# Layer 1's softmax divided by query, bfloat16 transposes by DMA, and expert biases carried in the weights

## The chip, the cores and the metric

The kernel runs as one program on one core of one Trainium2 chip. The metric is the device time of one execution in microseconds; three plain runs before the change took 1664.41, 1665.76 and 1665.9 us (median 1665.76). One more execution was recorded by the hardware profiler; all durations below are from it.

A core has five engines with a queue each, which run in the order of their queues and wait for one another through semaphores: PE (TensorE: matrix products and transposes, results in PSUM), DVE (VectorE), ACT (ScalarE), POOL (GpSimd) and SP (which here only issues DMAs).

## What is computed

Two layers on x of 2 x 2048 x 512, each a cross-attention to a context of 128 tokens and a feed-forward part, with a layer norm ahead of each and a residual. Cut to what the change touches:

```python
def _L0_ffn_ref(x, clip_x, clip_down, w_gate, w_up, w_down):
    # weights and activations are rounded to 255 steps: exact in bfloat16
    ...
def _L1_xattn_ref(q, k, v, mask, Wq, bq, Wk, bk, Wv, bv, Wo, bo):
    scores = jnp.einsum('bhqd,bhkd->bhqk', Q, K) / math.sqrt(DV)      # 16 heads of 32
    scores = jnp.where(mask, jnp.asarray(1e-09, scores.dtype), scores)
    attn = jax.nn.softmax(scores, axis=-1)
    ctx = jnp.einsum('bhqk,bhkd->bhqd', attn, V)
    return ctx.transpose(0, 2, 1, 3).reshape(b, -1, H * DV) @ Wo.T + bo
def _L1_ffn_ref(x, Wg, bg, We, be):
    probs = jax.nn.softmax(x @ Wg + bg, axis=-1)
    idx = jnp.argmax(probs, axis=-1)                                  # the expert: idx % 8
    p = jnp.take_along_axis(probs, idx[..., None], axis=-1)[..., 0]
    h = jax.nn.relu(jnp.einsum('bsd,edf->besf', x, We) + be[None, :, None, :])
    ...                                                               # the chosen expert's h times p
x = x + _L0_xattn_ref(_layernorm(x), ctx_1024, ctx_1024, ...)
x = x + _L0_ffn_ref(_layernorm(x), ...)
x = x + _L1_xattn_ref(_layernorm(x), ctx_1024, ctx_1024, ...)
x = x + _L1_ffn_ref(_layernorm(x), ...)
```

## The kernel before

The 4096 rows of x lie in SBUF as 32 tiles of 128 rows (`xs[n]`, with four more columns in `xw[n]`). The work runs in stages, one behind the other, with some overlap.

**Layer 0's attention (30 to 700 us)** is a loop over 64 units, a unit being 256 rows and 4 of 16 heads; its order on PE, DVE and ACT is that of the code (`manual_schedule`). Beside it the feed-forward weights are loaded by SP, rounded on DVE (`quantised`, L263 to L269), and one unit later transposed ("turns"): `gate_up` (22 tiles of 128 x 512) and `down` (4 of 128 x 1408) transpose in blocks of 128 x 128 on PE (L284, L302) and copy from PSUM on ACT (L285, L303).

**The feed-forward part, first half (711 to 870 us)**: 8 blocks of 512 rows, in each 11 steps of eight bfloat16 matmuls of 512 columns (L711), a Silu on ACT, a product and a maximum on DVE (L719, L721), and a store of h to DRAM by SP (L722). Between the steps DVE rounds the next block's rows (`quantised_x`, L95 and L666), PE transposes them (`turned_x`, L674), and ACT copies them to `xqT` (L675). Only PE's order is written out by hand here; a planner orders the other engines. Ahead of the blocks the gate's and the experts' biases are split into three bfloat16 parts each (`beparts`), with a table `sel` that selects an expert's rows.

**The second half** loads h back by SP, rounds it and multiplies by `wdT` (L777). It ends inside the first tile of layer 1. From here on PE, DVE, ACT and POOL all follow the order of the code.

**Layer 1's tiles (958 to 1488 us)**: for each of 32 tiles n the loop calls, with layer 1's feed-forward gate some tiles behind:
- `weighed(n-1)`: DVE multiplies tile n-1's mixed values by the reciprocal sums, L897
- `scores(n)`: PE, 16 products of 32 rows (L833); DVE masks (L841) and takes maxima (L846), 8 heads ("a half") at a time
- `queries`: PE (L813) and a copy on ACT (L816), for a later block; half of it here and half below
- `exponentials(n)`: ACT, one instruction per head (L855); those of the first half also sum, by accumulator
- `projected(n-1)`: POOL adds the output bias (L902), PE projects (L905), DVE adds to x (L906)
- `normed2(n-1)`, `kept_keys(n+1)`, `normed` of a later tile: statistics on DVE (L83, L85), a power on POOL (L92), the centering on DVE (L95)
- `logits(n-2)`: PE adds the bias by one bfloat16 product (L927) and multiplies by `wgate` (L929); DVE takes the maximum (L931) and its index (L935)
- `summed(n)`: DVE sums the second half (L859) and takes reciprocals (L861), POOL spreads them to features (`rw`, L864)
- `gated(n-2)`: an exponential on ACT (L943), the choice of the expert on DVE (L947 to L951)
- `turned(n)`: PE transposes the exponentials in four groups (L107) to PSUM, ACT copies them (L874)
- `turned2(n-1)`: the same for the normed x (L922)
- `mixed(n)`: PE transposes `rw` (L883), multiplies the exponentials by the values (L887); ACT copies the transposed `rw` (L892)
- `turned1`, in every second tile: PE and ACT transpose the next block's two tiles

PSUM tiles of the tag "m" share four banks, so the transposed groups, the logits, the projections and the queries take turns there: an allocation waits for the fourth one before it. From tile 24 on, `routing` sorts the rows of the first 22 tiles by expert on DVE, in pieces between the tiles.

**The experts (1463 to 1655 us)**: 39 calls of `expert(j)` on 128 rows each: rows gathered by POOL (L1096), centered on DVE, transposed on PE and copied on ACT (L1110), the bias added by one bfloat16 product (L1120), four products by the expert's weights (L1122, each two passes), a Relu on ACT (L1125), an addition on DVE (L1126), a scatter by POOL (L1127). Two of the calls lie in the last two tiles.

Of the kernel before, what the change touches and what calls it, by code (L numbers as in the profile page):

```python
# [11 lines left out]
F32 = mybir.dt.float32  # L12
# [11 lines left out]
P = 128  # L24
# [11 lines left out]
NE = 8  # L36
# [6 lines left out]
NJA = NTA - (NE - 1)  # L43
NJB = NT - NJA + NE - 1
NOWHERE = float(2**20)
QMAX = 127.0
# [12 lines left out]
def two_layers(ctx: ExitStack, tc: tile.TileContext, a, out):  # L59
# [14 lines left out]
    minus_half = const.tile([P, 1], F32, name="minus_half")  # L74
    nc.vector.memset(minus_half, -0.5)

    xw = [xres.tile([P, DX], F32, name=f"x{n}") for n in range(NT)]
# [64 lines left out]
    with ExitStack() as l0:  # L142
# [135 lines left out]
        def gate_up(w, dst, scales, i):  # L278
            wb = quantised(w, scales[:, i : i + 1])

            def turn():
                pt = psm.tile([P, ND, P], BF16, name="ptb", tag="m")
                for c in range(ND):
                    nc.tensor.transpose(pt[:, c, :], wb[:, c * P : (c + 1) * P], identb)  # L284
                nc.scalar.copy(dst[:, :, i * P : (i + 1) * P], pt)  # L285

            return turn
# [6 lines left out]
        def down(w, j):  # L294
            wb = quantised(w, sd[:, j : j + 1])

            def turn():
                for i in range(0, NI, 4):
                    n = min(4, NI - i)
                    pt = psm.tile([P, 4, P], BF16, name="ptb", tag="m")  # L300
                    for c in range(n):
                        nc.tensor.transpose(pt[:, c, :], wb[:, (i + c) * P : (i + c + 1) * P], identb)  # L302
                    nc.scalar.copy(wdT[:, i : i + n, j * P : (j + 1) * P], pt[:, :n, :])  # L303

            return turn
# [241 lines left out]
    wgate = wa.tile([P, ND, D], F32, name="wgate")  # L547
    beparts = w1.tile([P, D], BF16, name="beparts")
    sel = w1.tile([P, NE + 1, P], BF16, name="sel")
    bq = wa.tile([P, ND], F32, name="bq")  # L550
# [49 lines left out]
    with ExitStack() as up:  # L600
# [67 lines left out]
        def turned_x(n):  # L668
            blk, t = divmod(n, NBF)
            if t == 0:  # L670
                xqTs[blk] = work.tile([P, ND, BF], BF16, name="xqT", bufs=2)
            pt = psm.tile([P, ND, P], BF16, name="ptx", tag="m")
            for c in range(ND):
                nc.tensor.transpose(pt[:, c, :], xqs[n][:, c * P : (c + 1) * P], identb)  # L674
            nc.scalar.copy(xqTs[blk][:, :, t * P : (t + 1) * P], pt)  # L675
# [3 lines left out]
        for n in range(NBF):  # L679
            turned_x(n)  # L680

        nc.vector.memset(beparts, 0.0)
        nc.vector.memset(ones1, 1.0)
        nc.vector.tensor_scalar(bq, bq, 1.0 / math.sqrt(DH1), None, ALU.mult)
        bparts = kv.tile([NE + 1, 3, D], BF16, name="bparts")
        brest = kv.tile([NE + 1, D], F32, name="brest")
        load(brest[:NE, :], a["L1_ffn_be"])
        load(brest[NE:, :], a["L1_ffn_bg"].rearrange("(o d) -> o d", o=1))
        for k in range(3):
            nc.vector.tensor_copy(bparts[:, k, :], brest)  # L690
            nc.vector.tensor_tensor(brest, brest, bparts[:, k, :], ALU.subtract)
        be_dram = dram.tile([3, NE + 1, D], BF16, name="be_dram")
        nc.sync.dma_start(out=be_dram.rearrange("k e d -> e k d"), in_=bparts)
        for k in range(3):
            load(beparts[16 * k : 16 * k + NE + 1, :], be_dram[k])
        rowi = kv.tile([P, 1], I32, name="rowi")
        nc.gpsimd.iota(rowi, pattern=[[0, 1]], base=0, channel_multiplier=1)
        nc.vector.tensor_scalar(rowi, rowi, 15, None, ALU.bitwise_and)
        rowf = kv.tile([P, 1], F32, name="rowf")
        nc.vector.tensor_copy(rowf, rowi)  # L700
        ei_ = kv.tile([P, NE + 1], I32, name="ei_")
        nc.gpsimd.iota(ei_, pattern=[[1, NE + 1]], base=0, channel_multiplier=0)
        nc.vector.tensor_scalar(sel, ei_.unsqueeze(2).to_broadcast([P, NE + 1, P]), rowf, None, ALU.is_equal)

# [77 lines left out]

    scs, xTs, qTs, keeps, ss_, sums, rw_, pTs_, mix, os_ = {}, {}, {}, {}, {}, {}, {}, {}, {}, {}
    xn1s = {}
# [64 lines left out]
    def exponentials(n):  # L849

        sums[n] = small.tile([P, 16], F32, name="sums")
        for half, (s, mx) in enumerate(ss_[n]):
            for h in range(8):
                accum = {} if half else {"accum_out": sums[n][:, h : h + 1]}
                nc.scalar.activation(s[:, h, :], s[:, h, :], AF.Exp, bias=mx[:, h : h + 1], **accum)  # L855

    def summed(n):

        nc.vector.tensor_reduce(sums[n][:, 8:], ss_[n][1][0], AX.X, ALU.add)  # L859
        rs = small.tile([P, 4, 4], F32, name="rs")  # L860
        nc.vector.reciprocal(rs, sums[n].rearrange("p (r c) -> p c r", c=4))  # L861

        rw_[n] = mid.tile([P, 4, P], F32, name="rw", bufs=1)
        nc.gpsimd.tensor_copy(  # L864
            rw_[n].rearrange("p c (r f) -> p c r f", f=DH1), rs.unsqueeze(3).to_broadcast([P, 4, 4, DH1])
        )

# [9 lines left out]
    def mixed(n):  # L877

        b, pTs = n // TPB, pTs_[n]
        pr = psm.tile([P, 4, P], F32, name="pr1", tag="m")  # L880
        po = psm.tile([P, 4, P], F32, name="po1", tag="m")
        for c in range(4):
            nc.tensor.transpose(pr[:, c, :], rw_[n][:, c, :], ident)  # L883
        for c in range(4):
            for r in range(4):
                h = 4 * c + r
                nc.tensor.matmul(  # L887
                    po[32 * r : 32 * r + 32, c, :], v1[b][:, h * DH1 : (h + 1) * DH1], pTs[r][:, c, :],
                    start=True, stop=True, tile_position=(0, 32 * r),
                )  # L890
        oT = mid.tile([P, 4, P], F32, name="oT", bufs=1)
        nc.scalar.copy(oT, pr)  # L892
        mix[n] = po, oT

    def weighed(n):
        po, oT = mix[n]
        nc.vector.tensor_tensor(oT, po, oT, ALU.mult)  # L897
        os_[n] = oT

    def projected(n):  # L900

        nc.gpsimd.tensor_tensor(xs[n], xs[n], bob, ALU.add)  # L902
        pw = psm.tile([P, D], F32, name="pw1", tag="m")
        for c in range(ND):
            nc.tensor.matmul(pw, os_[n][:, c, :], wo1[:, c, :], start=(c == 0), stop=(c == ND - 1))  # L905
        nc.vector.tensor_tensor(xs[n], xs[n], pw, ALU.add)  # L906
# [12 lines left out]
    def turned2(n):  # L919
        pt = transposed(psm, xn2[n])  # L920
        xn2T[n] = mid.tile([P, ND, P], F32, name="xnT1", bufs=1)
        nc.scalar.copy(xn2T[n], pt)  # L922

    def logits(n):

        pl = pls[n] = psm.tile([P, D], F32, name="pl", tag="m")
        nc.tensor.matmul(pl, sel[:, NE, :], beparts, start=True, stop=False)  # L927
        for c in range(ND):
            nc.tensor.matmul(pl, xn2T[n][:, c, :], wgate[:, c, :], start=False, stop=(c == ND - 1))  # L929
        m8 = small.tile([P, 8], F32, name="m8")  # L930
# [7 lines left out]
    def gated(n):  # L938
# [11 lines left out]
        nc.vector.tensor_scalar(hot[:, n, :], iota_e, ef, None, ALU.is_equal)  # L950
        nc.vector.tensor_tensor(cum[:, n + 1, :], cum[:, n, :], hot[:, n, :], ALU.add)  # L951
        nc.vector.memset(xw[n][:, D + 3 : D + 4], 0.0)
# [153 lines left out]
    def turned_x2(j):  # L1106
        if j < NJ:
            pt = transposed(psm, part(6 + j % 3, [D]))
            ring[j] = part(9 + j % 3, [ND, P])
            nc.scalar.copy(ring[j], pt)  # L1110

    def expert(j):
# [5 lines left out]
        pz = psm.tile([P, D], F32, name="pz", tag="m")  # L1118

        nc.tensor.matmul(pz, sel[:, bass.ds(e, 1), :], beparts, start=True, stop=False)  # L1120
        for c in range(ND):
            nc.tensor.matmul(pz, ring[j][:, c, :], we[:, bass.ds(e, 1), c, :], start=False, stop=(c == ND - 1))  # L1122
        centered_x(j + 2)
# [39 lines left out]
    for n in range(NT):  # L1163
        blk, t = n // NB1, n % NB1
        ahead = blk + 1 < nblk
        fs = range(t * ND // NB1, (t + 1) * ND // NB1)
        if n > 0:
            weighed(n - 1)
        scores(n)
# [3 lines left out]
        if n == 0:  # L1173
            for i in range(NT - held, NT - held + 2):
                down(i)
                widened(i + 2)
        if n > 0:
            projected(n - 1)
            rest2 = normed2(n - 1)
# [3 lines left out]
        if n > 0:  # L1183
            rest2()
        if n > 1:
            logits(n - 2)
        summed(n)
        rest = gated(n - 2) if n > 1 else None
# [4 lines left out]
        if n == 0:  # L1193
# [6 lines left out]
            for e in range(NE):  # L1200
                load(we[:, e], a["L1_ffn_We"][e].rearrange("(c p) f -> p c f", p=P))
        if not ahead:

            expert(n - NT + NB1)
# [18 lines left out]
        if n == NT - NB1 - 1:  # L1223
            for j in range(2):
                centered_x(j)
            turned_x2(0)
    weighed(NT - 1)
    projected(NT - 1)
# [52 lines left out]
```

## Time and profile before

| what | us |
|---|---|
| three plain runs | 1664.41, 1665.76, 1665.9 |
| the profiled execution, its own time | 1666.03 |
| its span, first to last instruction | 1664.3 |
| layer 0's units, PE's step from one to the next | 9.79, 10.23, 10.45 or 12.14 |
| layer 1's tiles 2 to 23, scores to scores | 15.94 to 16.12 and 16.96 to 16.97 in turn |
| an expert (most of them) | 4.085 |
| granted TensorE clock | 0.998 of full speed |

The profile lists each instruction with its line, its engine, what it writes and reads, and how long it ran. In the rows in order of time the first number is the start in us from the span's start, the second the time that the row covers; "x4" is the number of instructions of the row, and the brackets hold the idle time of the engine ahead of the row and what ended it. PE stands for matrix products and transposes, PEld for the loads of their stationary operand, which overlap them. An fp32 product takes two instructions, a transpose one. Matmuls are pipelined: the step from one start to the next, not the duration, is what a matmul costs PE in a row of them.

### The profile page before, as it was taken

What the parts mean: (1) busy time and instruction counts of PE and PEld (TensorE: products, weight loads), DVE (VectorE), ACT (ScalarE), POOL (GpSimd) and SP (SyncE); (2) the same over time, 40 slices, a digit from 0 to 9 for tenths busy, and PEclk for the clock granted to TensorE, in tenths of its full rate; (3) what the DMA queues carried; (4) which work ended last, traced back from release to release, by engine and by line L of the source; (5) the groups of instructions that cost most, each with busy time, mean ns of one, the idle gap of its engine ahead of it and who ended that gap; (6) DMA issues with size and microseconds to landing.
All of it is one profiled execution on the core that took longest, in us unless ns stands there. A gap on an engine that the chain in (4) does not pass through costs nothing. (4 is left out here: it accounts for less than half of the span.)

```text
span 1664.3 us, 27098 instructions
## 1 busy us (share of the span) xinstructions
PE 1625.2 (98%) x10277; PEld 977.3 (59%) x10277; DVE 1176.4 (71%) x2294; ACT 709.4 (43%) x1601; POOL 390.8 (23%) x464
## 2 busy tenths in 40 slices
PE   7999999999999999999999999999999999999997
PEld 5666666666666555544444566676767666654553
DVE  3466667776667765699976678888888889875222
ACT  1223222222233222255445576666666666652222
POOL 2322222222222221100006632121211111224453
PEclk9999999999999999999999999999999999999999
DMA  9300000000000000455458750000000000113331
GB/s 331 132 15 18 20 14 20 14 20 14 20 14 8 35 18 1 141 146 158 146 155 282 248 202 15 20 21 14 20 14 20 14 21 14 46 46 103 124 118 62
DMA packets 89454, 118.24 MB, mean 71 GB/s; under 512 B 10732, under 2 KB 58146, under 8 KB 89325
## 3 DMA queue, kind: packets, MB, share of 16 engines
q1 hardware_dynamic: 80076, 96.63, 17.3%
q0 software_dynamic: 6240, 18.70, 3.5%
q8 instruction: 82, 1.34, 0.3%
q10 hardware_dynamic: 3008, 1.19, 0.3%
q14 instruction: 48, 0.39, 0.1%
HBM read 76.55 MB, written 41.77 MB: 71 GB/s over the span
## 5 line engine op out<-in xcount | busy, mean ns | idle before, releaser
L362 PE MATMUL pq<-xnT,wq 128*128 128x256 f32 x1024 | 254.4, 391 | 0.0
L420 PE MATMUL pw<-wo,att 128*128 128x512 f32 x512 | 230.8, 593 | 0.0
L362 PEld LDWEIGHTS pq<-xnT,wq 128*128 128x128 f32 x1024 | 184.4, 189 | 67.1 <-issue 38.7
L855 ACT ACTIVATE s<-s,mx 128x128 f32<-128x128 f32 x512 | 176.7, 387 | 18.0 <-DVE mx L846 18.0
L388 ACT ACTIVATE pr<-sc 128x1024 f32<-128x1024 f32 x64 | 65.9, 1030 | 237.0 <-PE sc L383 236.2
L420 PEld LDWEIGHTS pw<-wo,att 128*128 128x128 f32 x512 | 96.9, 190 | 96.4 <-issue 89.9
L410 DVE RECIPROCAL rd<-sc 128x256 f32<-128x256 f32 x64 | 112.5, 1758 | 51.3 <-PE sc L404 51.3
L372 POOL TENSOR_TENSOR q<-rt,rt 128x256 f32<-128x256 f32 x64 | 46.5, 727 | 422.4 <-DVE rt L371 422.4
L1122 PE MATMUL pz<-we,x 128*128 x312 | 140.3, 592 | 0.0
L367 DVE TENSOR_TENSOR rt<-pq,rope_cos 128x256 f32<-128x256 f32 x64 | 27.2, 425 | 141.2 <-PE pq L362 139.9
L347 ACT ACTIVATE xnT<-pt,lnb,lng 128x256 f32<-128x256 f32 x64 | 32.7, 561 | 216.2 <-PE pt L345 216.2
L813 PE MATMUL pq<-xT,wq 128*128 128x256 f32 x512 | 124.1, 385 | 0.0
L905 PE MATMUL pw<-wo,oT 128*128 128x512 f32 x256 | 115.5, 594 | 1.6 <-DVE oT L897 1.6
L929 PE MATMUL pl<-wgate,xnT 128*128 128x512 f32 x256 | 115.1, 592 | 0.0
L813 PEld LDWEIGHTS pq<-xT,wq 128*128 128x128 f32 x512 | 94.8, 190 | 28.1 <-issue 13.6
L1126 DVE TENSOR_TENSOR x<-x,x 128x512 f32<-128x512 f32 x39 | 27.0, 693 | 97.3 <-ACT x L1125 97.3
L841 DVE SCALAR_TENSOR_TENSOR s<-sc,keep 128x1024 f32<-128x1024 f32 x64 | 78.0, 1219 | 23.8 <-PE sc L833 23.8
L83 DVE BATCH_NORM_STATS2 st<-x 128x6 f32<-128x512 f32 x130 | 89.6, 689 | 6.0 <-DMA x<-in_ctx 3.7
L1122 PEld LDWEIGHTS pz<-we,x 128*128 128x128 f32 x312 | 58.9, 190 | 58.5 <-issue 56.8
L711 PE MATMUL pg<-xqT,wgT 128*128 128x512 bf16 x352 | 90.3, 379 | 0.7 <-ACT xqT L675 0.7
L711 PE MATMUL pu<-xqT,wuT 128*128 128x512 bf16 x352 | 90.3, 379 | 0.0
L716 ACT ACTIVATE gate<-pg,gsc 128x512 f32<-128x512 f32 x88 | 60.5, 687 | 68.9 <-PE pg L711 67.9
(229 smaller groups left out, 2888.9 us busy)
## 6 DMA issues: line engine op xcount, KB each, us to landing
h_dram<-h SPq DMA_DIRECT2D x88, 256.0 KB, 2.1
hq<-h_dram SPq DMA_DIRECT2D x31, 704.0 KB, 5.8
x_dram<-x SPq DMA_DIRECT2D x32, 258.0 KB, 3.0
x<-in_x SPq DMA_DIRECT2D x32, 256.0 KB, 5.7
we<-in_L_ffn_We SPq DMA_DIRECT2D x8, 1024.0 KB, 11.7
w_in<-in_L_ffn_w_gate SPq DMA_DIRECT2D x11, 256.0 KB, 2.6
w_down<-in_L_ffn_w_down SPq DMA_DIRECT2D x4, 704.0 KB, 4.1
w_in<-in_L_ffn_w_up SPq DMA_DIRECT2D x11, 256.0 KB, 2.6
```

The costliest lines, as they stand in the source:

```text
L83: nc.vector.bn_stats(out=st, in_=x)
L362: nc.tensor.matmul(pq, wqs[c // 2][:, c % 2, par, g * P : (g + 1) * P], xnTs[k][:, c, :], start=(c == 0), stop=(c == ND - 1))
L388: nc.scalar.activation(pr, sc[:, :, :B0], AF.Tanh, scale=1.0 / (math.sqrt(DH0) * GROK))
L410: nc.vector.reciprocal(rd, sc[:, 0, B0:])
L420: nc.tensor.matmul(pw, atts[u][:, f, t * P : (t + 1) * P], wo[:, 2 * g + f, :], start=(g == 0 and f == 0), stop=(g == NG - 1 and f == 1),)
L711: nc.tensor.matmul(dst, w[:, c, i * P : (i + 1) * P], xqTs[blk][:, c, :], start=(c == 0), stop=(c == ND - 1),)
L813: nc.tensor.matmul(pq, wq1[:, c, f * P : (f + 1) * P], xTs[blk][:, c, :], start=(c == 0), stop=(c == ND - 1))
L841: nc.vector.scalar_tensor_tensor(s, sc[:, 2 * half : 2 * half + 2].rearrange("p r c k -> p (r c) k"), -MASKED, keeps[n].unsqueeze(1).to_br ...
L855: nc.scalar.activation(s[:, h, :], s[:, h, :], AF.Exp, bias=mx[:, h : h + 1], **accum)
L905: nc.tensor.matmul(pw, os_[n][:, c, :], wo1[:, c, :], start=(c == 0), stop=(c == ND - 1))
L929: nc.tensor.matmul(pl, xn2T[n][:, c, :], wgate[:, c, :], start=False, stop=(c == ND - 1))
L1122: nc.tensor.matmul(pz, ring[j][:, c, :], we[:, bass.ds(e, 1), c, :], start=False, stop=(c == ND - 1))
```

## The change

Layer 1's attention: the exponentials of each query and head are now divided by their sum before they are transposed, in `shares`: half 0's sums by a reduction on DVE and the division by POOL, half 1's sums by ACT's accumulator and the division by DVE. `summed`, `weighed` and the transposes of `rw` go; ACT copies the mixed values from PSUM. POOL's addition of the output bias gets a call of its own (`biased`), and the count `cum` moves from DVE to POOL.

The biases of the gate and the experts: the products with `sel` and `beparts` go. Instead 4.0 is added to the first feature of each of the four transposed chunks (through the bias operand of ACT's copy), and each weight's matrices are lowered or raised by a row so that the four raised features bring in the bias. The row is worked out ahead (`vrow`), taken through DRAM and spread over 128 partitions (`rowadd`), and added to `wgate` by POOL in four instructions and to `we` by POOL in 32, two in each of the tiles 4 to 19.

The transposes of the rounded bfloat16 weights and of the rounded rows, the first block's excepted, become transposing DMAs on SP's queue.

```diff
+    raised = const.tile([P, 1], F32, name="raised")
+    nc.vector.memset(raised, 0.0)
+    nc.vector.memset(raised[:1, :], RAISE)
...
             def turn():
-                pt = psm.tile([P, ND, P], BF16, name="ptb", tag="m")
-                for c in range(ND):
-                    nc.tensor.transpose(pt[:, c, :], wb[:, c * P : (c + 1) * P], identb)
-                nc.scalar.copy(dst[:, :, i * P : (i + 1) * P], pt)
+                nc.sync.dma_start(out=dst[:, :, i * P : (i + 1) * P], in_=wb, transpose=True)
...
             def turn():
-                for i in range(0, NI, 4):
...
+                nc.sync.dma_start(out=wdT[:, :, j * P : (j + 1) * P], in_=wb, transpose=True)
...
+            if blk > 0:
+                nc.sync.dma_start(out=xqTs[blk][:, :, t * P : (t + 1) * P], in_=xqs[n], transpose=True)
+                return
...
+        vrow = kv.tile([nq, P], F32, name="vrow")
...
+        load(rowadd, v_dram[NE].partition_broadcast(P))
+        for c in range(ND):
+            nc.gpsimd.tensor_tensor(wgate[:, c, :], wgate[:, c, :], rowadd, ALU.add)
...
             for h in range(8):
-                accum = {} if half else {"accum_out": sums[n][:, h : h + 1]}
+                accum = {"accum_out": sums[n][:, 8 + h : 9 + h]} if half else {}
...
-    def summed(n):
...
+    def shares(n, half):
+
+        s, sm = ss_[n][half][0], sums[n][:, 8 * half : 8 * half + 8]
+        if half == 0:
+            nc.vector.tensor_reduce(sm, s, AX.X, ALU.add)
+        rs = small.tile([P, 8], F32, name="rs")
+        nc.vector.reciprocal(rs, sm)
+        engine = nc.vector if half else nc.gpsimd
+        engine.tensor_tensor(s, s, rs.unsqueeze(2).to_broadcast([P, 8, T]), ALU.mult)
...
-        for c in range(4):
-            nc.tensor.transpose(pr[:, c, :], rw_[n][:, c, :], ident)
...
-        oT = mid.tile([P, 4, P], F32, name="oT", bufs=1)
-        nc.scalar.copy(oT, pr)
-        mix[n] = po, oT
-
-    def weighed(n):
-        po, oT = mix[n]
-        nc.vector.tensor_tensor(oT, po, oT, ALU.mult)
-        os_[n] = oT
+        os_[n] = mid.tile([P, 4, P], F32, name="oT", bufs=1)
+        nc.scalar.copy(os_[n], po)
+
+    def biased(n):
+        nc.gpsimd.tensor_tensor(xs[n], xs[n], bob, ALU.add)
...
-        nc.scalar.copy(xn2T[n], pt)
+        nc.scalar.activation(xn2T[n], pt, AF.Identity, bias=raised)
...
-        nc.tensor.matmul(pl, sel[:, NE, :], beparts, start=True, stop=False)
...
-        nc.vector.tensor_tensor(cum[:, n + 1, :], cum[:, n, :], hot[:, n, :], ALU.add)
+        nc.gpsimd.tensor_tensor(cum[:, n + 1, :], cum[:, n, :], hot[:, n, :], ALU.add)
...
-            nc.scalar.copy(ring[j], pt)
+            nc.scalar.activation(ring[j], pt, AF.Identity, bias=raised)
...
-        nc.tensor.matmul(pz, sel[:, bass.ds(e, 1), :], beparts, start=True, stop=False)
...
-        if n > 0:
-            weighed(n - 1)
         scores(n)
...
         if n > 0:
+            biased(n - 1)
+        shares(n, 0)
+        if n > 0:
             projected(n - 1)
             rest2 = normed2(n - 1)
...
         if n > 0:
             rest2()
+        shares(n, 1)
         if n > 1:
             logits(n - 2)
-        summed(n)
         rest = gated(n - 2) if n > 1 else None
...
+        if 4 <= n < 4 + 2 * NE:
+            e, half = divmod(n - 4, 2)
+            if half == 0:
+                load(rowadd, v_dram[e].partition_broadcast(P))
+            for c in range(2 * half, 2 * half + 2):
+                nc.gpsimd.tensor_tensor(we[:, e, c, :], we[:, e, c, :], rowadd, ALU.add)
```

## The prediction

> **What bounds the kernel now.** I read the shares of the engines first, then the order in time of one tile of layer 1, then the lengths of all 32 tiles, the units of layer 0, the blocks of the feed-forward stage and the experts. Every time below is of the one profiled execution: 1666.03 us, a span of 1664.3 and 1.7 around it. The median of the three plain runs is 1665.76 (1664.41 to 1665.9), 0.3 lower, so the sum carries over as it is.
>
> ```profile
> PE 1625.2 (98%) x10277; PEld 977.3 (59%) x10277; DVE 1176.4 (71%) x2294; ACT 709.4 (43%) x1601; POOL 390.8 (23%) x464
> ```
>
> PE is busy nearly always, so whatever leaves PE seems to be gain. That holds where nothing else arrives at the same moment. One tile of layer 1, in order of time:
>
> ```profile
> 1204.35 1.17 PE L833 MATMUL sc<-kT,qT 32*128 32x128 f32 x32
> ...
> 1209.23 1.22 DVE L846 TENSOR_REDUCE mx<-s 128x8 f32<-128x1024 f32 x1
> ...
> 1210.99 0.69 DVE L906 TENSOR_TENSOR x<-x,pw 128x512 f32<-128x512 f32 x1 [0.53 <-PE pw L905]
> ...
> 1211.26 2.43 ACT L855 ACTIVATE s<-s,mx 128x128 f32<-128x128 f32 x8
> ...
> 1213.93 0.54 DVE L95 TENSOR_SCALAR xn<-x,mv 128x512 f32<-128x512 f32 x1
> ...
> 1214.09 0.78 POOL L92 TENSOR_TENSOR r<-ve,minus_half 128x1 f32<-128x1 f32 x1 [0.59 <-DVE ve L91]
> ...
> 1215.44 0.69 DVE L935 FIND_INDEX8 i<-m,pl 128x8 uint32<-128x512 f32 x1
> ...
> 1216.05 1.20 DVE L859 TENSOR_REDUCE sums<-s 128x8 f32<-128x1024 f32 x1
> ...
> 1216.17 0.66 ACT L943 ACTIVATE sc<-pl,negm 128x512 f32<-128x512 f32 x1 [2.48 <-DVE i L935]
> ...
> 1216.85 0.47 ACT L816 ACTIVATE qT<-pq,bq 128x256 f32<-128x256 f32 x1
> ...
> 1217.20 2.05 ACT L874 COPY s<-pt 128x512 f32<-128x512 f32 x4
> ...
> 1218.27 1.29 POOL L902 TENSOR_TENSOR x<-x,bob 128x512 f32<-128x512 f32 x1
> 1218.36 1.21 DVE L951 TENSOR_TENSOR cum<-cum,hot 128x8 bf16<-128x8 bf16 x1
> ...
> 1218.97 1.39 PE L887 MATMUL po<-s,v 128*32 128x128 f32 x32
> ...
> 1219.30 0.79 PEld L887 LDWEIGHTS po<-s,v 128*32 128x32 f32 x26 [0.18 <-ACT s L874]
> ```
>
> A second chain ends together with PE. Call the start of a tile's scores S (1204.35 here). DVE works in the written order down to the index search, which ends at S+11.78. ACT had waited 2.48 us for that to run gated's exponential. Behind it in ACT's queue stand a qT copy and the four copies of the transposed exponentials (2.05); PE's mixed waits for the last copy (0.18); 4.16 us after the search PE is free for the next scores, or for turned1, which takes another 1.03 in every second tile. The tiles last 15.94 and 16.97 us in turn. That the search, not PE, sets the end is shown by a tile into which the routing puts more DVE work:
>
> ```profile
> 1369.14 1.17 PE L833 MATMUL sc<-kT,qT 32*128 32x128 f32 x32
> ...
> 1381.79 0.69 DVE L935 FIND_INDEX8 i<-m,pl 128x8 uint32<-128x512 f32 x1
> ...
> 1382.52 0.66 ACT L943 ACTIVATE sc<-pl,negm 128x512 f32<-128x512 f32 x1 [1.65 <-DVE i L935]
> ...
> 1383.35 1.09 PE L107 MATMUL pt<-ident,s 128*128 128x128 f32 x8 [0.42 <-ACT sc L943]
> ...
> 1387.66 1.17 PE L833 MATMUL sc<-kT,qT 32*128 32x128 f32 x32
> ```
>
> Its search ends 1.56 us later than usual and the tile is 1.55 longer (18.52 against 16.97). PE waits at the third transpose, for ACT's exponential, whose PSUM bank it needs.
>
> **Layer 0: -12.5 us.** A unit of PE's work lasts 9.79, 10.23 where xn is transposed in it, 10.45 with the four bf16 transposes of a gate or up tile, 12.14 with the eleven of a down tile (there PE also waits 0.89 for ACT). So 22 x 0.22 = 4.8 and 4 x 1.92 = 7.7. PE has no other waiter close: q is ready 0.5 us before PE reaches the scores. The 26 transposes go to SP and wait there for wb; behind them stand the next weights' loads, which have a unit of time, as SP's queue now waits 458 us in all for wb's maker. The transposed weights are needed a stage later.
>
> **Feed-forward: -5 us.** PE streams 88 steps of 1.725 and 28 groups of transposes of 0.22 in 158.2 us without a gap. 28 x 0.22 = 6.2 leave it. DVE needs 11 x 1.38 + 4 x 0.8 = 18.4 us of a block's new 19.0, so the gain is 6.2 at best; POOL's four wgate additions (1.28 each, L902) run where POOL was idle, but hold DVE's casts at times: between -6.2 and 0, I take -5, near the first because PE was the only full engine. The trace has no transposing DMA. Below, a 256 KB store from SBUF lands in 2.1 us (h_dram); above, bq's 2 KB in 4-byte pieces take 6.4. The last xq of a block is cast some 20 us before that block (829.9 against 850.8), so four transposes behind one another are hidden up to about 4.7 us each; I take no stall, nearest to the store. On SP the stores of h stand behind a transpose that waits for xq, but xq is that early, and h has four buffers. [...]
>
> **Experts: -8.4 us.** An expert is 4.085 us, PE without a gap; the bias matmul (L1120) starts 0.215 before the next. 37 experts behind the tiles and two logits: 39 x 0.215. ACT idles 2.9 us in each, so its bias costs nothing.
>
> **Layer 1's tiles: +91 us.** PE loses 0.46 (pr) and 0.21 (bias) a tile, some 21 us in all. By busy time DVE loses too: weighed 22.1 and cum 33.1 go, 32 multiplications of about 1.2 and reciprocals come. But those that go lay behind the search, and those that come lie ahead of it:
> - Maxima end at S+6.10. The first half's exponentials, now without sums, take the 2.43 of the old second half: from S+3.81 to 6.24. Then reduce 1.20 and reciprocal 0.2: x+pw starts at 7.75 instead of 6.64. **+1.1**
> - POOL multiplies half 0 from 7.75. L372 takes 0.73 for 256 elements and L902 1.28 for 512, so 1024 take about 2.4: to 10.1. A DVE operation of the kind that needs POOL idle waits for it: cum (1.21 beside L902, 0.16 at 1467.34 with POOL free). keep, at 9.55, is of tensor_scalar form, and normed2's power queues behind the multiplication. xn2 moves from x+pw + 2.94 to about 11.3. **+0.6** (0 to 1.7, if the multiplication stretches as L780 does from 1.27 to 1.85)
> - Reciprocal 0.17, POOL's second power (0.78), multiplication of half 1 (1.22, twice a 0.69 less its start): **+1.4**. Max and search: 1.56 as before, to about S+14.95.
>
> So the search ends 3.1 us later (2.4 without both holds, 4.2 with the stretch), and the 4.16 behind it stay: the exponential, qT and the copies queue behind it on ACT, PE waits for those. PE would reach the third transpose at S+12.5 and go on at 15.9. n=2 to 27: 26 x 3.1 = 80.6. n=28, 29 lack one norm: 2 x 2.5. n=30, 31 (with experts): 2 x 3.2. n=0 and 1: 1.6. The routing's DVE work fits in the time for which DVE now waits: -2.5. Sum 91. What is moved to POOL besides (biased, cum, 32 additions on we: 41 us in tiles 4 to 19) lies behind the search, where POOL and DVE wait over 4 us; the we loads and rowadd loads have SP nearly to themselves there.
> The new 3.4 us gap on PE: the trace has a wait of 7.8 us (for xn at the start) in a stretch of granted clock 1.00, so I charge nothing. [...]
>
> **Sum:** -12.5 - 5 - 8.4 + 91 = +65: 1666 + 65 = **1731**. All ends low: 2.4 a tile gives 70 - 27 = +43, 1709; all high: 4.2 a tile and nothing from the feed-forward stage, 124 - 21 = +103, 1769.
>
> **Rivals.**
> - *Faster: the DVE work is covered, PE stays the bound.* If the exponential L943 no longer held PE's third transpose nor the copies on ACT, every PE removal would count: 12.5 + 6.2 + 8.4 + 21 = 48, **1618**. For it: PE's 98% and DVE's lower sum. Against: the routing tile, 1.56 to 1.55. It decides if the search ends, with the 0.9 of the exponential, before PE reaches the third transpose at S+12.5. Chance 0.12.
> - *The transposing DMAs are slow*, on top of the forecast: each us beyond 4.7 costs 4 us at each of 7 block changes, 28 us; at 7 us each, +64: **1795**. For it: 512 pieces of 4 bytes took 6.4 us. Chance 0.10.
> - *The parts cancel*: 1 us a tile, because the reduction or the multiplication hides behind waits that I count as gone (x+pw waited 0.53 for PE): about **1666**. Chance 0.03.
> - Forecast: 0.75.
>
> The range leaves out the faster case, the cancelling one and the far ends: 1695 to 1790. Faster by over 0.2% (what a measurement of this kernel can tell) 0.12, within 0.03, slower 0.85.
>
> **What would show it.** Tiles of 18.5 to 20 us; ACT's wait for the index search near 5 us instead of 2.48; PE waiting some 3 us at the third transpose; PE's share down to about 91% (1625 less 48, of 1730). Units of layer 0 at 10.23, block steps without a gap, experts at 3.87. It is wrong if tiles stay below 16.5, or if PE waits for xqT at the block changes.

## The result and the profile after

| | us |
|---|---|
| before, median of four runs | 1665.22 (1664.41 to 1665.9) |
| changed, median of four runs | 1741.25 (1739.34 to 1742.51) |
| ratio | 1.0456, 95% interval 1.0438 to 1.0474 |
| forecast | 1731, range 1695 to 1790 |
| profiled executions, their spans | 1664.3 before, 1737.5 changed |

The changed kernel is 4.6% slower, and the forecast was 10 us short. The 73.2 us between the two spans lie in these stages, read from the starts of PE's rows:

| stretch | before | changed | difference | forecast |
|---|---|---|---|---|
| start to the first product of the feed-forward part | 711.59 | 698.14 | -13.45 | -12.5 |
| first to last of its products (L711) | 157.33 | 156.34 | -1.0 | -5 |
| from there to layer 1's first scores | | | -1.0 | |
| first scores to the third expert | 537.94 | 633.83 | +95.9 | +91 |
| third expert to the end | | | -7.3 | -8.4 |

The page's shares of the engines:

```profile
PE 1621.1 (93%) x9834; PEld 964.7 (56%) x9834; DVE 1165.5 (67%) x2290; ACT 692.7 (40%) x1539; POOL 489.4 (28%) x530
```

PE and DVE both have less to do, and the kernel is longer: no engine's sum explains it, a wait does. A tile of layer 1, n = 16, in order of time; the one shown of before is its neighbour n = 15, but before the change the search ends at S+11.78 in both. S is 1252.87 here; L861 and L865 are `shares`, L898 is x + product, L103 the centering, L926 the index search, L934 the gated exponential, L115 the transposes.

```profile
1252.87 1.17 PE L833 MATMUL sc<-kT,qT 32*128 32x128 f32 x32
...
1259.24 1.22 DVE L861 TENSOR_REDUCE sums<-s 128x8 f32<-128x1024 f32 x1 [0.19 <-ACT s L855]
...
1260.61 0.65 DVE L898 TENSOR_TENSOR x<-x,pw 128x512 f32<-128x512 f32 x1
...
1260.86 1.90 POOL L865 TENSOR_TENSOR s<-s,rs 128x1024 f32<-128x1024 f32 x1 [8.30 <-ACT s L855]
...
1262.37 0.47 DVE L823 TENSOR_SCALAR keep<-masks 128x128 f32<-128x128 uint8 x1
...
1263.77 0.54 DVE L103 TENSOR_SCALAR xn<-x,mv 128x512 f32<-128x512 f32 x1
1263.93 0.78 POOL L100 TENSOR_TENSOR r<-ve,minus_half 128x1 f32<-128x1 f32 x1 [0.67 <-DVE ve L99]
...
1264.45 1.22 DVE L865 TENSOR_TENSOR s<-s,rs 128x1024 f32<-128x1024 f32 x1
...
1266.45 0.69 DVE L926 FIND_INDEX8 i<-m,pl 128x8 uint32<-128x512 f32 x1
1267.18 0.66 ACT L934 ACTIVATE sc<-pl,negm 128x512 f32<-128x512 f32 x1 [4.85 <-DVE i L926]
...
1268.01 1.97 PE L115 MATMUL pt<-ident,s 128*128 128x128 f32 x8 [2.57 <-ACT sc L934]
...
1269.77 1.06 PE L115 MATMUL pt<-ident,xn 128*128 128x128 f32 x4
...
1270.76 1.27 PE L883 MATMUL po<-s,v 128*32 128x128 f32 x32
...
1271.96 1.17 PE L833 MATMUL sc<-kT,qT 32*128 32x128 f32 x32
```

The search ends at S+14.27 instead of S+11.78, 2.49 us later; ACT waits 4.85 us for it, PE then 2.57 for ACT, and the tile lasts 19.09, where n = 16 lasted 15.94 before. Over the sixteen tiles 4 to 19 the mean is 19.60 us, against 16.46 before: 3.14 more. That leaves 0.65 beyond the search of this tile (0.59 by the means, since the searches of the sixteen tiles end 2.55 later), and the row of PE behind the wait shows where: eight transposes take 1.97 us, while the eight ahead of the wait (1264.40) take 1.04. The granted clock in windows of one us (window, length, busy PE, clock, DMA share, GB/s):

```profile
1266.00:1267.00 1.00, 0.00 (x0) 1.00 0.00 0
1267.00:1268.00 1.00, 0.00 (x0) 0.90 0.00 0
1268.00:1269.00 1.00, 0.99 (x5) 0.50 0.00 0
1269.00:1270.00 1.00, 1.00 (x7) 0.50 0.69 264
1270.00:1271.00 1.00, 1.00 (x12) 0.50 0.00 0
1271.00:1272.00 1.00, 1.00 (x36) 0.90 0.00 0
```

The clock halves for 0.2 + 3 + 0.2 = 3.4 us. From 1180 to 1270 us this came behind four of the five waits.

### The profile page after: what moved, and what is told of

Read it like the earlier page. It is cut to its first block, busy times and chain, and to the rows that moved or that the text cites. A ratio compares the mean times of both kernels' runs of the same rounds, so it can differ in the third digit from the quotient of the medians.

```text
span 1737.5 us, 26326 instructions
## 1 busy us (share of the span) xinstructions
PE 1621.1 (93%) x9834; PEld 964.7 (56%) x9834; DVE 1165.5 (67%) x2290; ACT 692.7 (40%) x1539; POOL 489.4 (28%) x530
## 3 DMA queue, kind: packets, MB, share of 16 engines
q8 instruction: 78, 1.28, 0.3%
## 5 line engine op out<-in xcount | busy, mean ns | idle before, releaser
L115 PE MATMUL pt<-ident,s 128*128 128x128 f32 x512 | 76.8, 298 | 81.6 <-ACT sc L934 77.6
L865 POOL TENSOR_TENSOR s<-s,rs 128x1024 f32<-128x1024 f32 x32 | 60.7, 1896 | 284.4 <-ACT s L855 283.9
L115 PEld LDWEIGHTS pt<-ident,s 128*128 128x128 f32 x512 | 63.4, 152 | 94.5 <-ACT sc L934 84.6
L716 ACT ACTIVATE gate<-pg,gsc 128x512 f32<-128x512 f32 x88 | 60.5, 687 | 95.9 <-PE pg L711 87.5
L711 PE MATMUL pu<-xqT,wuT 128*128 128x512 bf16 x352 | 91.2, 382 | 3.3 <-DVE h L719 3.3
```

The costliest lines, as they stand in the source:

```text
L115: nc.tensor.transpose(pt[:, c, :], src[:, c * P : (c + 1) * P], ident)
L711: nc.tensor.matmul(dst, w[:, c, i * P : (i + 1) * P], xqTs[blk][:, c, :], start=(c == 0), stop=(c == ND - 1),)
```

## The experiments

My theory: DVE's work that the change puts ahead of the index search holds the gated exponential on ACT, this PE's third group of transposes, and the wait then costs PE its clock. Rivals: POOL's new additions collide with the tiles; the same DVE work costs the same wherever it stands; the slow transposes cost nothing; the search is not what the exponential waits for. All kernels, in us; the tile is the mean of tiles 4 to 19, the wait is the median of PE's waits ahead of the third group in those tiles (in filler_two ahead of the products put there), the clock that of 1000 to 1480 us:

| kernel | median | ratio to before, 95% | tile | wait | clock |
|---|---|---|---|---|---|
| changed | 1741.25 | 1.0456 (1.0438 to 1.0474) | 19.60 | 2.57 | 0.94 |
| softmax_alone | 1760.51 | 1.057 (1.0552 to 1.0588) | 19.58 | 2.36 | 0.94 |
| rest_alone | 1640.19 | 0.9848 (0.9831 to 0.9864) | 16.25 | none | 1.00 |
| half1_late | 1727.15 | 1.0371 (1.0354 to 1.0388) | 19.21 | 2.50 | 0.94 |
| filler_two | 1784.89 | 1.0709 (1.0691 to 1.0727) | 21.14 | 2.58 | 0.96 |
| filler_early | 1724.4 | 1.0356 (1.0339 to 1.0374) | 19.02 | 0.92 | 1.00 |
| sums_act | 1718.54 | 1.0321 (1.0303 to 1.0338) | 18.79 | 2.19 | 0.97 |
| exp_first | 1719.93 | 1.0329 (1.0312 to 1.0347) | 18.85 | 2.26 | 0.95 |
| keep_late | 1699.53 | 1.0211 (1.0195 to 1.0226) | 18.11 | 1.74 | 1.00 |
| all_kept | 1673.81 | 1.0055 (1.0039 to 1.007) | 17.43 | 1.43 | 1.00 |
| wgate_late | 1737.57 | 1.0437 (1.042 to 1.0455) | 19.60 | | 0.94 |
| row_own | 1740.46 | 1.0456 (1.0439 to 1.0474) | 19.61 | | 0.94 |
| rest_late | 1633.61 | 0.9814 (0.98 to 0.9827) | 16.25 | none | 1.00 |

### The parts apart

**softmax_alone**: before, with `shares`, `biased` and the new `mixed`, and none of the rest.

> The kernel before with the softmax part of the change alone. My theory, that the division ahead of the index search lengthens the tile, expects the whole growth of the change's tiles here and a little more, since the gate's bias product (0.22 us a tile) stays: before + 93 to 103, about 1763 us, tiles of 19.4 to 20 us, the gated exponential waiting some 5 us for the index search. The rival, that the growth is a collision with the biases' additions on POOL or with other new work of the change, expects tiles of at most 18 us and 1665 + 45 = 1710 or less.

The tile is that of the changed kernel, 19.58, with no addition to weights on POOL, and the total + 95.1. From the list of waits (total us, times, longest):

```profile
ACT sc L935 <- DVE i L927: 158.6, 32, 9.1
```

It is 157.5 us in the changed kernel and was 84.3 before. A collision with POOL's additions is not needed for the growth.

**rest_alone**: the changed kernel with the softmax of before.

> The change without its softmax part: transposing DMAs and biases in the weights only, softmax as in the kernel before. My theory expects layer 0's 13.5 us, the experts' 7.3 us and FFN's 1.0 us to be won as in the changed kernel, and up to 0.22 us in each of 30 tiles (at most 6.6): 1665.2 - 22 to - 28, so 1637 to 1643 us. The rival, that the additions on POOL slow the tiles in which they stand (n = 4 to 19), expects those tiles above 17.5 us and no gain or a loss, 1650 to 1670.

The total fell by 25.2, inside the forecast. The tiles with POOL's additions are as long as the ones behind them, 15.75 and 16.76 in turn, and PE has no wait in them. So the change is one part that loses 95 us and others that together win 25. They do not quite add up: 95.1 - 25.2 = 69.9, where the whole change costs 76.0. The tiles explain the 6 us: without the gate's bias product they are 0.2 us shorter in rest_alone (16.25 against 16.46), about 6 us in 30 tiles, but the changed kernel's, which lack it too, are as long as those of softmax_alone, which have it (19.60 and 19.58).

### What the tile waits for

**half1_late**: the second half's division goes behind the search.

```diff
-        shares(n, 1)
         if n > 1:
             logits(n - 2)
         rest = gated(n - 2) if n > 1 else None
+        shares(n, 1)
```

> The changed kernel with the second half's reciprocal and multiplication (0.23 + 1.22 us on DVE) moved from ahead of the gate's maximum and index search to behind them. My theory, that what stands on DVE ahead of the search sets the third group of transposes, expects the search 1.45 us earlier, and the tile shorter by that less what the second half's multiplication then holds the same transposes: 0.6 to 1.45 us a tile, 18 to 44 us in all, so 1697 to 1723, about 1705. The rival, that the same DVE work costs the same wherever it stands, or that POOL or the clock makes the tile, expects 1736 to 1746.

One tile, whose scores start at 1250.08:

```profile
1262.29 0.69 DVE L926 FIND_INDEX8 i<-m,pl 128x8 uint32<-128x512 f32 x1
...
1263.02 0.66 ACT L934 ACTIVATE sc<-pl,negm 128x512 f32<-128x512 f32 x1 [3.48 <-DVE i L926]
...
1263.78 1.23 DVE L865 TENSOR_TENSOR s<-s,rs 128x1024 f32<-128x1024 f32 x1
...
1265.15 1.06 PE L115 MATMUL pt<-ident,s 128*128 128x128 f32 x8 [2.50 <-ACT s L873]
```

The search ends 1.37 us earlier, at S+12.90, as forecast. But PE starts the third group at S+15.07 instead of S+15.14. The group reads the second half, whose multiplication now ends at 1265.01; the profile names ACT's copy, whose end falls at the same time. My lower bound of 0.6 us had taken that end too early, without most of the small DVE operations between the two (0.76 us). The time missed its range by 4 us. By this two things hold the third group, the search and that multiplication, so DVE's whole work up to there counts, not its order alone; that it is the multiplication and not the copy is read from the code and the times, not tested.

**exp_first**: the search behind the exponential.

```diff
-        nc.vector.max_index(out=i8, in_max=m8, in_values=pl)
...
         nc.scalar.activation(
             scs[min(n + 2, NT - 1)][:, 0]..., pls[n], AF.Exp, bias=negm, accum_out=pe
         )
+        nc.vector.max_index(out=i8, in_max=m8, in_values=pls[n])
```

> The changed kernel with the index search put behind the gated exponential, which reads the same product, so that the exponential waits for the maximum and its sign alone (0.73 us of search and value load less). My theory, that the search releases the exponential and this the third group of transposes: PE's wait of 2.6 us falls to 1.9, tiles 0.7 us shorter, up to 1.4 where PE keeps its clock: 22 to 42 us, 1699 to 1720. If the exponential waited for something else that comes at the same time, 1738 to 1744.

A tile whose scores start at 1245.07:

```profile
1258.69 0.66 ACT L932 ACTIVATE sc<-pl,negm 128x512 f32<-128x512 f32 x1 [4.17 <-DVE negm L924]
...
1259.37 0.46 ACT L816 ACTIVATE qT<-pq,bq 128x256 f32<-128x256 f32 x1
...
1259.89 1.97 PE L115 MATMUL pt<-ident,s 128*128 128x128 f32 x8 [2.26 <-ACT qT L816]
```

The exponential now waits for the sign of the maximum and starts at S+13.62 instead of S+14.31. PE's wait shrinks by 0.31 only, because the third group here starts when ACT's qT copy ends, 0.36 us behind the exponential. The time is 21.3 lower, at the edge of what was expected; how much of the rest of it is clock, this run does not separate.

**sums_act**: DVE's reduction taken away, its work given to ACT's accumulators.

```diff
-                accum = {"accum_out": sums[n][:, 8 + h : 9 + h]} if half else {}
+                accum = {"accum_out": sums[n][:, 8 * half + h : 8 * half + h + 1]}
...
-        if half == 0:
-            nc.vector.tensor_reduce(sm, s, AX.X, ALU.add)
```

and `shares(n, 0)` behind `projected(n - 1)`.

> The changed kernel with the first half's sums taken by ACT's accumulators as well, so that DVE's reduction (1.22 us) goes, and with that half's reciprocal behind the addition of the projected product. If DVE's work ahead of the index search sets the tile, x + product starts right behind its product on PE, 1.1 us earlier, the search too, and the tile is 1.0 to 1.2 us shorter, with up to 0.7 more where the shorter wait of PE keeps its clock: 1741 - 31 to - 57, 1684 to 1710 us. If ACT's exponentials (8 accumulators more, 0.8 us) or POOL's multiplication set the third group of transposes, 1736 or slower.

It gained 22.7 where 31 to 57 were expected. x + product did start 1.1 us earlier (S+6.64), but two rows behind it:

```profile
1251.91 1.90 POOL L863 TENSOR_TENSOR s<-s,rs 128x1024 f32<-128x1024 f32 x1 [7.92 <-DVE rs L861]
1252.74 1.15 DVE L823 TENSOR_SCALAR keep<-masks 128x128 f32<-128x128 uint8 x1
```

keep ends where POOL's multiplication ends (1253.8), 1.15 us instead of the 0.22 of before: it gives back 0.68 of the 1.1 compared with the 0.47 of the changed kernel.

**keep_late**: sums_act, with `kept_keys(n + 1)` moved behind `gated(n - 2)`.

> The changed kernel with all sums by ACT's accumulators and x + product ahead of the first reciprocal, and besides with the keep mask of the next tile moved from between the two norms to behind the index search. In the run without that move keep took 1.15 us, ending with POOL's multiplication, instead of 0.22. If POOL's multiplication is what lengthens it, keep takes 0.2 to 0.25 us at its new place, where POOL multiplies nothing. What it frees is then worth only 0.4 us a tile, because POOL's own power for the norm still stands behind the multiplication and is next: 1718.5 - 12, 1703 to 1710. If DVE's time alone counted, 1.15 us a tile, 1684. If keep is long for a reason of its own, it stays above 1 us.

From the list of that operation (ns: least, median, most):

```profile
L823 DVE TENSOR_SCALAR keep<-masks x32: 214/223/225, 941.6 to 1504.5; 128x128 f32<-128x128 uint8 x32
```

In the changed kernel the three are 175, 473 and 759. So it is POOL's multiplication that stretches keep. Another 0.68 us a tile went, and the total fell by 19.0 to 3.5 us below the expected range. The search accounts for 0.45 of the 0.68 (S+13.44 instead of 13.89, means of the sixteen tiles), close to the 0.4 expected; for the rest PE's wait is down to 1.74 and the clock at 1.00 from 1000 us on, instead of 0.97.

### The clock

**filler_two**: two products of 128x512 that nobody reads, between the second and the third group of transposes, into the last bank of the scores.

> The changed kernel with two useless matrix products of 128x512 (0.9 us each) between the second and the third group of transposes of every tile, where PE waits 2.6 us; their result is never read, and the output is unchanged. If the half clock after that wait costs time, it goes: granted clock 1.00 instead of 0.94 from 1000 to 1540 us, the third group's eight transposes 1.04 us in every tile, tiles shorter by 0.5 to 0.7 us, in all 15 to 21 us, 1720 to 1726. The rival, that the slow transposes lie beside ACT's copies and cost nothing, expects 1738 to 1744 with the clock at 1.00 all the same; and if the wait was not what lowers the clock, it stays at 0.94 and the time as well.

It was 43.6 us slower, which I had not foreseen, because the filler waited itself:

```profile
PE sc L873 <- ACT sc L937: 73.2, 28, 4.1
```

The gated exponential writes into another bank of the same tile of scores, so the products queue behind it, and PE's wait stays (2.58) with 1.8 us of work behind it. It says nothing on the clock's price.

**filler_early**: the same products ahead of the exponential in the order.

```diff
         if n > 1:
             logits(n - 2)
+            for c in range(2):
+                nc.tensor.matmul(scs[n][:, 3].rearrange("p c k -> p (c k)"), ident, wq1[:, c, :], start=True, stop=True)
         rest = gated(n - 2) if n > 1 else None
```

> The changed kernel with two useless matrix products of 128x512 (0.9 us each) right behind the gate's product, so that PE's 2.6 us wait ahead of the third group of transposes shrinks to about 0.8 us; nothing reads their result. If the half clock after the wait costs what the slow transposes show, tiles become 0.5 to 0.7 us shorter although PE has 1.8 us more to do: 15 to 21 us, 1720 to 1726 us, granted clock 0.98 or more from 1000 to 1540 us (0.94 without them). If the slow transposes lie beside ACT's copies, the clock rises and the time stays, 1736 to 1746. If PE's own work counts, it is 30 x 1.8 = 54 us slower, about 1795.

The windows of 1000 to 1500 us (PE, PEld, DVE, ACT, POOL busy, then the clock), first of the changed kernel, then of this one:

```profile
1000.00:1500.00 500.00, 433.06 (x3028) 288.72 (x3027) 356.93 (x742) 278.56 (x899) 161.41 (x158) 0.94 0.05 18
```

```profile
1000.00:1500.00 500.00, 472.41 (x3260) 300.95 (x3259) 366.32 (x766) 284.12 (x918) 166.75 (x164) 1.00 0.06 20
```

The third group of a tile whose scores start at 1245.57:

```profile
1260.76 1.09 PE L115 MATMUL pt<-ident,s 128*128 128x128 f32 x8 [0.92 <-ACT sc L934]
```

With 1.8 us more for PE in each tile the kernel is 16.9 us faster, and the tile 0.58 shorter. The search ends at S+14.30 and the third group starts at S+15.22, where the changed kernel has 14.34 and 15.21 (means of the sixteen tiles), so what became shorter lies behind them. That is the price of the half clock, shown: 0.58 of the 0.59 us that the searches left open. From 1180 to 1270 us, waits of 2.57 us (the changed kernel) brought the half clock four times in five and waits of 2.19 us (sums_act) twice in five, while those of 1.74, 1.43 and 0.92 us (the medians of keep_late, all_kept and filler_early) left the clock at 1.00. The half clock comes in stretches of 3.413 us (a few are twice as long), and within a run they start whole multiples of 3.413 us apart: in the changed kernel at 1189.28, 1209.76, 1230.24 and 1267.79, which is 6, 6 and 11 of them.

How much idle time it takes can be read by cutting the time from 1000 to 1480 us at these multiples and adding up PE's idle time in each piece, in all eleven kernels of the table that have a wait. Of the pieces at full clock, 113 had 1.99 to 3.30 us of it, and half clock followed each; 1306 had at most 2.01 us, and it followed none; of these the changed kernel has 16 with 2.24 to 3.29 us and 107 with at most 1.94. So in these kernels some 2 us of idle time inside one piece were enough. A wait counted as far as it fell into one piece: of the changed kernel's five waits of 2.57 us four put 2.24 to 2.35 us into one, and the fifth, which ends at 1248.56, put 1.33 us into one and 1.25 into the next, without half clock behind it. A wait of 1.74 us is below 2 wherever it falls.

### The feed-forward part

**wgate_late**: the four additions to `wgate` moved from this stage to layer 1's second tile.

> The changed kernel with the four additions to the gate's weights on POOL (5.3 us) moved from FFN's first stretch to layer 1's second tile. If they hold DVE there, the one stall of PE in FFN (2.85 us, and 2.3 us of half clock behind it) goes, and FFN's first to last product takes 152 to 153.5 us instead of 156.3: 1736 to 1738 us in all. The rival, that the stores of h behind four transposing DMAs of 1.2 us each in SP's queue make the stall, expects 156 to 157 us there and 1740 to 1742 in all.

First to last product took 152.63 us, and PE's stall of 2.7 us at 720.84 was gone: nearly all of the forecast -5 was there to be had (157.33 - 152.63 = 4.7). A second stall, 0.57 us at 737.07 in the changed kernel, stayed and was longer:

```profile
734.30 1.02 PE L709 MATMUL pu<-xqT,wuT 128*128 128x512 bf16 x4 [1.38 <-DVE h L717]
```

The reading that POOL's additions hold DVE's casts was too quick, though. SP's queue in the changed kernel:

```profile
706.19 0.50 SPq L74 DMA_DIRECT2D rowadd<-v_dram  x1
706.78 1.49 SPq L722 DMA_DIRECT2D h_dram<-h  x2
715.71 0.34 SPq L74 DMA_DIRECT2D rowadd<-v_dram  x1
716.14 6.41 SPq L722 DMA_DIRECT2D h_dram<-h  x6
```

The load of the first expert's row, needed in layer 1's fifth tile, was ordered here. It goes into the buffer that POOL is still reading for the gate (until 715.7), SP waits for that, and four stores of h queue up (the row's other two, at 720.81 and 722.19, are of products made later). All four buffers of h are then full, as the next rows of DVE and PE show:

```profile
720.04 0.75 DVE L719 SCALAR_TENSOR_TENSOR h<-pu,usc,gate 128x512 f32<-128x512 f32 x1 [2.72 <-DMA h_dram<-h]
...
720.84 1.10 PE L711 MATMUL pu<-xqT,wuT 128*128 128x512 bf16 x4 [2.68 <-DVE h L719]
```

The move had taken the additions and this load away together, so it could not tell them apart.

**row_own**: the additions in their place, with a buffer of their own for the gate's row.

> The changed kernel with a buffer of its own for the gate's row, everything else in its place. In SP's queue of the changed kernel the load of the first expert's row stands in FFN's first stretch, from 708.3 to 715.7 us waiting for POOL's four additions, because it goes into the same buffer; six stores of h queue behind it, and PE's one stall in FFN ends when a store has landed. If that queue is the cause, the stall and the half clock behind it go although POOL adds at the same place: FFN's first to last product 152 to 153.5 us, 1736 to 1738 in all. If POOL's additions make the stall by holding DVE's casts (1.47 and 0.81 us beside them instead of 0.41 and 0.53), FFN stays at 156 to 157 us and the whole at 1740 to 1742.

Neither number came as the queue theory had it: 156.15 us, and 1740.46 in all. The load no longer waits, but it still stands there:

```profile
706.44 0.50 SPq L74 DMA_DIRECT2D rowgate<-v_dram  x1
706.99 0.63 SPq L74 DMA_DIRECT2D rowadd<-v_dram  x1
707.71 13.26 SPq L723 DMA_DIRECT2D h_dram<-h  x8
```

```profile
714.26 0.75 DVE L720 SCALAR_TENSOR_TENSOR h<-pu,usc,gate 128x512 f32<-128x512 f32 x1 [1.80 <-DMA h_dram<-h]
```

DVE again waits for a store of h. POOL's additions start at 711.79, and the casts ahead of the stall run unhindered (0.41 and 0.54 us), so they are not its cause. The stores now stand behind two rows of 256 KB each instead of one. But this wait costs PE only some 1.0 us, over three steps of 1.99, 2.03 and 2.16 us instead of 1.73; the stall that the waiting load made, and the half clock behind it, are gone, as the queue theory has it. What kept the time is the second stall:

```profile
735.44 0.93 PE L712 MATMUL pu<-xqT,wuT 128*128 128x512 bf16 x2 [2.10 <-DVE h L720]
```

It has grown from 0.57 to 2.10 us, and now the clock halves behind this one, at 735.56. DVE waits 2.30 us there, once more for a store of h; in SP's queue four transposes and a load of 704 KB for the second half (`wq<-h_dram`) stand ahead of those stores. That load is there before the change as well, where DVE waited 2.91 us behind it and PE not at all. Why the second stall is 0.57, 1.38 and 2.10 us in the three kernels is not shown; a kernel with only the load of the first expert's row moved was not run.

### What is left of the softmax part, and the best version

**all_kept**: sums_act, keep_late, exp_first and wgate_late together.

> The changed kernel with all four repairs: sums by ACT, keep behind the search, the search behind the gated exponential, and the additions to the gate's weights behind FFN. If the gains add, 1718.5 - 12 - 22 - 4, about 1680 us, and more where PE's wait becomes short enough to keep its clock (30 tiles by up to 0.7: 1660). My theory, that DVE's multiplication and POOL's hold on the norm stay on the path, expects PE still to wait 0.8 us or more at the third group of transposes, tiles of 17 us or more against 16.25 without the softmax part, so 1660 to 1685: slower than 1636 in any case. The rival, that the softmax part pays once these waits are gone, since it takes 0.63 us of transposes from PE, expects 1636 or less.

```profile
1267.87 1.10 PE L115 MATMUL pt<-ident,s 128*128 128x128 f32 x8 [1.42 <-ACT qT L814]
```

Tiles of 17.43 us, with 1.42 of waiting left and the clock whole. The four edits took 67.4 us off, 0.7 from the sum of what they brought one by one (22.7 + 19.0 + 21.3 + 3.7 = 66.7). DVE's multiplication of the second half (1.22) and the norm's wait of 0.52 for POOL still lie ahead of the search, and the kernel is still slower than before.

**rest_late**: rest_alone and wgate_late.

> The change without its softmax part and with the additions to the gate's weights moved behind FFN. The two are in different stages, so their gains should add: 1640.2 us of the first, less the 4.4 us that FFN's first to last product became shorter by the second (157.1 to 152.6), about 1636 us, ratio 0.982 to the kernel before. If the additions cost as much in layer 1's second tile, whose PE has no gap in this kernel, 1640.

1633.61 us, 2.4 below the sum expected: faster than both kernels, 0.9814 of before (0.98 to 0.9827). The softmax part, the best of it that was tried, costs 1673.81 - 1633.61 = 40 us on top of it, although it takes PE's transposes of `rw` away.

## Why the forecast was right in its direction, point by point

- **What bounds the kernel.** Right. The index search sets the end of a tile through ACT's exponential and the third transpose: moving DVE work ahead of it lengthened the tile, removing it shortened it. That "the search, not PE, sets the end" holds for the changed kernel; before, the search itself waited for PE: DVE's maximum ahead of it waited 0.10 us for the gate's product, and with 0.2 us of PE's work less in rest_alone the search ended at S+11.59 instead of 11.78 and the tile 0.2 earlier.
- **Layer 0, -12.5.** Right to the figure: units of 9.79 and 10.23 throughout; of the stage's other 0.95, 1.3 were won ahead of the units and 0.4 lost behind them. The 26 transposing DMAs held nobody.
- **Feed-forward, -5.** Wrong, -1.0. The failing step is "h has four buffers", by which I let SP's queue be harmless. I had counted the transposes in that queue but not the loads of the new rows, one of which the planner ordered into this stage; the second stall, 0.57 us, stands behind a load that was there before. Behind the first stall the clock halved too (four products 1.91 us instead of 1.03). The transposing DMAs were no slower than assumed: two take 2.52 us of SP, 1.26 for each, and DVE waited for them eight times, 2.7 us in all, without PE.
- **Experts, -8.4.** Mechanism right, 3.87 us each as forecast; the first few are bound by other waits, hence -7.3.
- **Tiles, x + product, +1.1.** Right: S+7.74, forecast 7.75.
- **Tiles, POOL's hold, +0.6.** Too large: 0.2. POOL multiplies in 1.90 us, not 2.4, and keep overlapped it by 0.25 only. In sums_act the same hold cost 0.93: the mechanism is as forecast, the size depends on when POOL starts.
- **Tiles, second half, +1.4.** Near: 1.17 (S+10.90 for the centering to 14.27 for the search's end, less the 2.20 of before). DVE's tensor_tensor multiplication ran beside POOL's power in 1.22 us, unhindered.
- **"The 4.16 behind it stay", and the 3.4 us wait charged with nothing.** Wrong: it was 4.82 in the tile shown, by the half clock. The wait of 7.8 us, from which I argued, was not followed by full clock. The clock's record begins only at 17.3 us, and a stretch without a record reads as 1.00; PE's rows show otherwise: the products `pk` start every 0.43 us up to 16.9 us and every 0.215 us from 17.3 on. So the profile of before already held the price that I put at nothing. In the changed kernel the wait was 2.57 us, and filler_early shows 0.58 us a tile for the clock that it cost.
- The two errors in the tile (0.6 too much for DVE, 0.65 too little for the clock) cancelled, so the tiles' +91 came near +95.9 partly by luck. Most of the miss of 8 us between the spans (73.2 against 65) is these 5 and the feed-forward part's 4.
- **Rivals.** Faster by DVE being covered: its condition, the exponential early enough for PE, was never met with the new softmax, not even with four repairs (1.42 us of waiting left). Slow transposing DMAs: PE has no wait at a block change. Cancelling parts: the 1 us a tile that it wanted was 3.1.

## What to carry to other kernels

An operation that moves across engines is to be placed on the chain that ends last: here less work on PE and on DVE made the kernel longer, since the new DVE work stood ahead of the one instruction that others wait for. A wait that is put before PE had a second price here from some 2 us on (0.58 us a tile for waits of 2.57), so price it by the clock as well, and test it with useless products in the gap. A new load counts in its queue where the planner puts it, not where the code writes it.

## What was not expected of the hardware

- The clock halved for 3.4 us behind many of PE's waits of 2.2 to 2.6 us, never behind 1.7 us. Within a run it did so whole multiples of 3.413 us apart, after each full-clock piece between them with more than some 2 us of idle time.
- POOL's multiplication with a broadcast operand took 1.90 us for 1024 elements a partition, less than by the rows of before (0.73 for 256, 1.28 for 512). Beside it DVE's tensor_scalar on keep ended when POOL ended (0.22 to 1.15 us), while the bn statistics (0.69) and tensor_tensor with PSUM (0.65) kept their times.
- Useless work on PE made the kernel 16.9 us faster.
